# A mixture-of-experts router: small VectorE operations taken out, moved to GpSimd and folded into matmuls

## The chip, the cores and the metric

The kernel runs on one core of a Trainium2 chip. The metric is the device time of one execution in microseconds; lower is better. The core has five engines that run their own instruction streams and wait for one another by semaphores: TensorE (PE, matrix products), VectorE (DVE), ScalarE (ACT), GpSimd (POOL) and SyncE (SP, which here only issues DMAs). Each engine works strictly in the order of its stream, so an instruction that waits holds up all behind it.

## The reference

A block of a transformer in three parts works on 4096 tokens of 256 features: half a feed-forward network, an attention over groups of 64 tokens, and half a feed-forward network again with the same weights. The feed-forward network is a mixture of experts with a shared part:

```python
xn = xf * rsqrt(mean(xf * xf) + eps)              # RMS norm of each token
logits = xn @ router_w.T                          # 8 experts
probs = softmax(logits)
topk_p, topk_i = top_k(probs, 2)                  # two experts for each token
rw = topk_p / sum(topk_p)                         # their weights
order = argsort(~sel, axis=1, stable=True)        # tokens of an expert, in order
dispatch = order[:, :capacity]                    # at most 640 of them
eout = einsum(silu(xg @ rg) * (xg @ ru), rd)      # the expert
routed = zeros.at[dispatch].add(eout * w)
shared = silu(x @ sg) * (x @ su) @ sd
return shared + routed
x = x + 0.5 * ffn(layernorm(x)); x = x + attn(layernorm(x)); x = x + 0.5 * ffn(layernorm(x))
```

The weights of the two experts depend only on the difference of the two largest logits: with d = exp(second - first) they are 1/(1+d) and d/(1+d). The choice of the experts doesn't depend on a positive factor common to a token's logits. A token's place in an expert's list is the number of earlier tokens with the same expert.

## The kernel before

Four stages follow one another: `a` (norm and routing of all tokens for the first network, the shared part of the first four blocks), `b` (the eight experts), `c` (the attention of all tokens, the rest of the shared part, and norm and routing for the second network), `d` (the experts again and the last shared block). A tile is 128 tokens, a block four tiles (512 tokens).

A float32 value is carried as two 16-bit parts, a high and a low one; a product takes the three terms of `TERMS` (high by high, high by low, low by high), added up in one PSUM buffer. `split` makes the two parts of a weight, scaled by `WS` = 16; `project` writes the 3 x 2 matmuls of a product of depth 256.

The shared part (`shared`, `gate_up`, `down`) is what TensorE does most of: for each block 16 chunks, each 12 + 12 matmuls on `pgu` (L306), the activation on ScalarE and VectorE (`sl` L313, L314, L319; `hh` L321, `hl` L322), and 12 matmuls on `po` (L330). The tiles are generators that `drive` runs in small steps between the steps of the shared part. The order that is written down in this way is then planned by the framework's scheduler: it places the instructions on each engine by its own estimate of when each could start. So a change in one place moves other instructions too. Scatters are told to come after the POOL instruction in `self.anchor`.

For each tile, `front_steps` computes mean and variance (L139 to L144; the power on POOL gives `rstd`), the normed tile `X` in two 16-bit parts, transposes it into `xb`, and calls `logits`. There the router weights `rwt` hold their high part in columns 0 to 7 and their low part, scaled by `UP` = 2048, in columns 8 to 15; four matmuls with 16 columns (L207) go through both, and DVE adds the two halves (`q` L211, `L` L212).

When four tiles are there, `route` runs once for the block, in steps:

- the RMS factor `rs` (DVE L220 to L222, the power on POOL L223), and `L` times `rs` (L226);
- the largest values of each tile and their indices (`mx`, `ix` L230, L231), the difference `dl` (L233), its exponential on POOL (L234), the indices as floats `ef` (L236);
- a one-hot `oh` of both choices (L239) and their sum `M` (L243); `C` holds, for each tile of the block, the counts of all tiles before it, partition by partition (L245, L247), `run` the total to date (L248);
- two matmuls on `pp`: a triangle of ones by `M` counts inside the tile (L251), a square of ones by `C` all earlier tiles (L252); VectorE picks the positions (`pk`, `pos` L254, L257), makes the target rows (`df` L260 to L264) and casts them to integers `di` (L266);
- the two weights `w1` and `dl` (L268 to L272);
- for each tile, `scatter`: POOL copies token number, weights and expert into the tile's tag columns (L285) and issues two indirect DMAs (L287) that write the tile's rows to the lists `xg` of the experts.

In stage `c` a tile first goes through the attention (`attn_tile`), and its POOL work shares the queue with the scatters: `ss` (L501, the power for the norms of q and k, which VectorE's `qk` L511 needs), the low parts `xa`, `QK`, `yp`, `e` (L165, L522, L528, L561) and the subtraction of the maximum `S` (L550). The buffers `X` are freed by the scatters; a stage has 10 in `a` and 6 in `c`.

Of the kernel before, what the change touches and what calls it, by code (L numbers as in the profile page):

```python
# [8 lines left out]
F32 = mybir.dt.float32  # L9
F32R = mybir.dt.float32r  # L10
F16 = mybir.dt.float16
BF16 = mybir.dt.bfloat16
# [3 lines left out]
ALU = mybir.AluOpType  # L16
AX = mybir.AxisListType
# [3 lines left out]
P = 128  # L21
# [3 lines left out]
UP = 2048.0  # L25
WS = 16.0
# [3 lines left out]
E = 8  # L30
CAP = 640
LN_EPS = 1e-5
RMS_EPS = 1.1920929e-07
SUBS = ((0, 384), (384, 256))
TERMS = ((0, 0), (0, 1), (1, 0))


class Net:
    def __init__(self, ctx, tc):
        self.tc = tc  # L40
        self.nc = nc = tc.nc
        pool = lambda name, bufs, **k: ctx.enter_context(tc.tile_pool(name=name, bufs=bufs, **k))
        self.cst = pool("cst", 1)
        self.wsh = pool("wsh", 1)
        self.tok = pool("tok", YB)
        self.xb = pool("xb", NB)
        self.xe = pool("xe", 2)
        self.sm = pool("sm", 2)
        self.dr = pool("dr", 1, space=DRAM)
        self.ps_gu = pool("ps_gu", 3, space=PSUM)  # L50
        self.pend = None
        self.anchor = None
        c = self.cst
        self.tri = c.tile([P, P], BF16, name="tri")
        nc.gpsimd.memset(self.tri, 1.0)
        nc.gpsimd.affine_select(
            out=self.tri, in_=self.tri, pattern=[[1, P]], compare_op=ALU.is_gt,
            fill=0.0, base=0, channel_multiplier=-1)
        self.ones = c.tile([P, P], BF16, name="ones")
        nc.gpsimd.memset(self.ones, 1.0)  # L60
        self.iota8 = c.tile([P, E], F32, name="iota8")
        for e in range(E):
            nc.gpsimd.memset(self.iota8[:, e:e + 1], float(e))
        self.mhalf = c.tile([P, 8], F32, name="mhalf")
        nc.gpsimd.memset(self.mhalf, -0.5)
        self.e1 = c.tile([P, 4], F32, name="e1")
        nc.gpsimd.memset(self.e1, 2.718281828459045)
        tk = self.sm.tile([P, 32], I32, name="tk", bufs=1)
        nc.gpsimd.iota(tk, pattern=[[P, 32]], base=0, channel_multiplier=1)
        self.tokid = c.tile([P, 32], F32, name="tokid")  # L70
        nc.vector.tensor_copy(self.tokid, tk)
# [32 lines left out]
    def load_router(self, router_w):  # L104
        nc = self.nc
        r = self.raw.tile([E, H], F32, name="rtr", tag="raw2")
        nc.sync.dma_start(out=r, in_=router_w)
        self.rwt = self.cst.tile([P, 2, 2 * E], F16, name="rwt")
        p = self.m1([P, 2, E], F32, "prt")
        for k in range(2):  # L110
            nc.tensor.transpose(p[:, k, :], r[:, k * P:(k + 1) * P], self.ident[:E, :E])
        z = self.sm.tile([P, 2, E], F32, name="rz", bufs=1)
        nc.vector.tensor_scalar_mul(z, p, UP)
        nc.scalar.mul(self.rwt[:, :, 0:E], z, 1.0 / UP)
        nc.vector.scalar_tensor_tensor(
            out=self.rwt[:, :, E:2 * E], in0=self.rwt[:, :, 0:E], scalar=-UP, in1=z, op0=ALU.mult, op1=ALU.add)

    def load_shared(self, sg, su, sd):

# [82 lines left out]
    def logits(self, fb, t, xt):  # L202

        nc = self.nc
        p = self.m1([P, 2 * E], F32, "pl")
        for a in range(4):
            nc.tensor.matmul(p, lhsT=xt[:, a, :], rhs=self.rwt[:, a % 2, :], start=(a == 0), stop=(a == 3))  # L207
        if t == 0:
            fb["L"] = self.sm.tile([P, 4, E], F32, name="L")
        q = self.sm.tile([P, E], F32, name="q")  # L210
        nc.vector.tensor_scalar_mul(q, p[:, E:2 * E], 1.0 / UP)  # L211
        nc.vector.tensor_tensor(out=fb["L"][:, t, :], in0=q, in1=p[:, 0:E], op=ALU.add)  # L212

    def route(self, R, b, fb):

        nc = self.nc
        sm = self.sm
        mv, rstd = fb["mv"], fb["rstd"]
        rs = sm.tile([P, 4], F32, name="rs")
        nc.vector.tensor_tensor(out=rs, in0=rstd, in1=rstd, op=ALU.mult)  # L220
        nc.vector.tensor_tensor(out=rs, in0=rs, in1=mv[:, :, 1], op=ALU.mult)
        nc.vector.tensor_scalar_add(rs, rs, RMS_EPS * UP ** 2)  # L222
        nc.gpsimd.tensor_tensor(out=rs, in0=rs, in1=self.mhalf[:, :4], op=ALU.pow)  # L223
        yield
        L = fb["L"]
        nc.vector.tensor_tensor(out=L, in0=L, in1=rs.unsqueeze(2).to_broadcast([P, 4, E]), op=ALU.mult)  # L226
        mx = sm.tile([P, 4, E], F32, name="mx")
        ix = sm.tile([P, 4, E], U32, name="ix")
        for t in range(4):
            nc.vector.max(out=mx[:, t, :], in_=L[:, t, :])  # L230
            nc.vector.max_index(out=ix[:, t, :], in_max=mx[:, t, :], in_values=L[:, t, :])  # L231
        dl = sm.tile([P, 4], F32, name="dl")
        nc.vector.tensor_tensor(out=dl, in0=mx[:, :, 1], in1=mx[:, :, 0], op=ALU.subtract)  # L233
        nc.gpsimd.tensor_tensor(out=dl, in0=self.e1, in1=dl, op=ALU.pow)  # L234
        ef = sm.tile([P, 4, 2], F32, name="ef")
        nc.vector.tensor_copy(ef, ix[:, :, 0:2])  # L236
        yield
        oh = sm.tile([P, 4, 2, E], F32, name="oh")
        nc.vector.tensor_tensor(  # L239
            out=oh, in0=ef.unsqueeze(3).to_broadcast([P, 4, 2, E]),  # L240
            in1=self.iota8.unsqueeze(1).unsqueeze(1).to_broadcast([P, 4, 2, E]), op=ALU.is_equal)
        M = sm.tile([P, 4, E], BF16, name="M")
        nc.vector.tensor_tensor(out=M, in0=oh[:, :, 0, :], in1=oh[:, :, 1, :], op=ALU.add)  # L243
        C = sm.tile([P, 4, E], BF16, name="C")
        nc.vector.tensor_copy(C[:, 0, :], R["run"])  # L245
        for t in range(3):
            nc.vector.tensor_tensor(out=C[:, t + 1, :], in0=C[:, t, :], in1=M[:, t, :], op=ALU.add)  # L247
        nc.vector.tensor_tensor(out=R["run"], in0=C[:, 3, :], in1=M[:, 3, :], op=ALU.add)  # L248
        yield
        pp = self.m1([P, 4, E], F32, "pp")  # L250
        nc.tensor.matmul(pp, lhsT=self.tri, rhs=M, start=True, stop=False)  # L251
        nc.tensor.matmul(pp, lhsT=self.ones, rhs=C, start=False, stop=True)  # L252
        pk = sm.tile([P, 4, 2, E], F32, name="pk")
        nc.vector.tensor_tensor(  # L254
            out=pk, in0=oh, in1=pp.unsqueeze(2).to_broadcast([P, 4, 2, E]), op=ALU.mult)
        pos = sm.tile([P, 4, 2], F32, name="pos")
        nc.vector.tensor_reduce(out=pos, in_=pk, axis=AX.X, op=ALU.add)  # L257
        yield
        df = sm.tile([P, 4, 2], F32, name="df")
        nc.vector.scalar_tensor_tensor(  # L260
            out=df, in0=ef, scalar=float(CAP), in1=pos, op0=ALU.mult, op1=ALU.add)
        nc.vector.tensor_scalar(
            out=pos, in0=pos, scalar1=float(CAP), scalar2=8192.0, op0=ALU.is_ge, op1=ALU.mult)
        nc.vector.tensor_tensor(out=df, in0=df, in1=pos, op=ALU.add)  # L264
        di = sm.tile([P, 4, 2], I32, name="di")
        nc.vector.tensor_copy(di, df)  # L266
        w1 = sm.tile([P, 4], F32, name="w1")
        nc.vector.tensor_scalar_add(w1, dl, 1.0)  # L268
        nc.vector.reciprocal(w1, w1)
        nc.vector.tensor_scalar_mul(w1, w1, 0.5 / WS)  # L270
        nc.vector.tensor_tensor(out=dl, in0=dl, in1=w1, op=ALU.mult)
        nc.vector.tensor_tensor(out=w1, in0=w1, in1=dl, op=ALU.subtract)  # L272
        yield
        for t in range(4):
            with self.tc.issue_after(self.anchor.ins) if self.anchor else nullcontext():
                self.scatter(R, b, fb, t, di, w1, dl, ef)
            yield
# [552 lines left out]
```

## Time and profile before

| | before |
|---|---|
| median of 3 runs | 1857.15 us (1856.97 to 1858.42) |
| profiled execution | 1854.02 us |
| its span | 1852.2 us |
| TensorE busy | 1785.9 us (96%) |
| VectorE busy, instructions | 1259.6 us (68%), 3190 |
| ScalarE busy | 940.6 us (51%) |
| GpSimd busy | 726.0 us (39%) |

The profile is of one execution. A line of a group or of the timeline names the line of the kernel, the engine, the operation, output and inputs by the program's names, partitions x elements and type. In the timeline the first two columns are start and duration in microseconds, and the brackets hold the idle time of the engine before the instruction and what ended it. In the table of waits the columns are the total in microseconds, the number of times, and the longest.

### The profile page before, as it was taken

The numbers are of one execution on the slowest core, as the hardware profiler recorded it, in microseconds if no ns is written. First come the engines' busy times: TensorE is split into PE (matmuls) and PEld (weight loads), VectorE is DVE, ScalarE is ACT, GpSimd is POOL, SyncE is SP. The second block draws the span as 40 slices with busy tenths as digits, with TensorE's granted clock in tenths as the row PEclk, the third lists the DMA queues.
The fourth block names the chain that finished last, engine by engine and source line by source line (L and its number), as shares of the span: only waits on it lengthen the run. The fifth ranks groups of instructions, "written<-read, shape, count | busy, mean of one in ns | idle before, by whom it ended". The sixth has DMA issues, their size and how long they took to land.

```text
span 1852.2 us, 37412 instructions
## 1 busy us (share of the span) xinstructions
PE 1785.9 (96%) x13546; PEld 1189.7 (64%) x13546; DVE 1259.6 (68%) x3190; ACT 940.6 (51%) x1991; POOL 726.0 (39%) x943
## 2 busy tenths in 40 slices
PE   6899999999999899999999999999999999999999
PEld 3456557777777556665555656565665677777765
DVE  8666545566666567888888888788765566666643
ACT  4333334555555466666566666666433455555542
POOL 5664430123111334557667575757520011112210
PEclk9999999999999999999999999999999999999999
DMA  9763032555543345657576666756213044445420
GB/s 272 220 161 93 12 78 61 114 121 116 119 107 86 82 81 101 135 104 146 103 140 122 130 130 115 147 104 122 53 34 83 27 106 111 110 109 125 106 47 12
DMA packets 447513, 196.59 MB, mean 106 GB/s; under 512 B 302369, under 2 KB 444381, under 8 KB 447264
## 3 DMA queue, kind: packets, MB, share of 16 engines
q1 hardware_dynamic: 429664, 173.03, 41.6%
q0 software_dynamic: 17664, 21.17, 6.7%
q8 instruction: 106, 1.74, 0.4%
q14 instruction: 79, 0.65, 0.1%
HBM read 81.04 MB, written 52.85 MB: 72 GB/s over the span
## 4 chain that ended last, share of the span: by engine, by line
PE 59%; DVE 11%; POOL 9%; DMA 8%; issue 6%; ACT 4%; SPq 1%; DVEq 0%; POOLq 0%; ACTq 0%
PE pgu L306 38%; PE po L330 19%; POOL xg L287 3%; DVE hl L322 2%; DVE sl L319 2%; DMA xg<-X,di 2%; DVE sl L314 2%; DMA xg<-zero 1%; DMA y<-in_L_attn_x_dram 1%; DMA rs<-in_L_ffn_su_dram 1%; POOL X L285 1%; ACT hh L321 1%; DMA QT<-QK 1%; DVE st L139 1%; ACT V L554 1%
## 5 line engine op out<-in xcount | busy, mean ns | idle before, releaser
L306 PE MATMUL pgu<-xb,sgu 128*128 128x512 f16 x3072 | 740.2, 381 | 19.5 <-DVE sl L314 8.5
L321 ACT CAST hh<-sl 128x512 f16<-128x512 f32 (+2 forms) x512 | 272.8, 533 | 540.8 <-DVE sl L319 535.5
L306 PE MATMUL pgu<-xe,wc 128*128 128x384 f16 (+1 forms) x3072 | 497.1, 299 | 0.6
L306 PEld LDWEIGHTS <-sgu 128*128 128x128 f16 x3072 | 294.1, 98 | 298.1 <-issue 33.0
L319 DVE SCALAR_TENSOR_TENSOR sl<-pgu,sl 128x512 f32<-128x512 f32 (+2 forms) x512 | 300.6, 587 | 203.4 <-PE pgu L306 183.2
L322 DVE TENSOR_TENSOR hl<-sl,hh 128x512 f16<-128x512 f32 (+2 forms) x512 | 328.4, 642 | 146.4 <-ACT hh L321 145.4
L330 PEld LDWEIGHTS <-hh 128*128 128x128 f16 x3328 | 319.6, 98 | 114.8 <-ACT hh L321 18.4
L330 PE MATMUL po<-sdw,hh 128*128 128x256 f16 x2048 | 350.6, 273 | 10.8 <-ACT hh L321 10.0
L306 PEld LDWEIGHTS <-wc 128*128 128x128 f16 x3072 | 300.1, 98 | 94.6 <-issue 2.2
L330 PE MATMUL po<-sdw,hl 128*128 128x256 f16 x1024 | 250.9, 274 | 11.4 <-DVE hl L322 10.6
L330 PE MATMUL po<-wd,hh 128*128 128x256 f16 x1280 | 223.7, 273 | 0.0
L330 PEld LDWEIGHTS <-hl 128*128 128x128 f16 x1664 | 162.6, 98 | 62.3 <-DVE hl L322 28.5
L426 POOL DMA_INDIRECT out_dram<-eo,eid x40 | 64.6, 1616 | 315.2 <-DVE hl L322 247.1
L317 ACT ACTIVATE sl<-pgu 128x384 f32<-128x384 f32 (+1 forms) x336 | 158.8, 473 | 53.8 <-PE pgu L306 30.4
L287 POOL DMA_INDIRECT xg<-X,di x128 | 137.3, 1072 | 89.4 <-DVE di L266 29.9
L426 POOL DMA_INDIRECT acc<-eo,eid x40 | 64.6, 1615 | 261.9 <-DVE hl L322 222.3
L330 PE MATMUL po<-wd,hl 128*128 128x256 f16 x640 | 152.5, 273 | 1.1 <-DVE hl L322 1.1
L314 DVE SCALAR_TENSOR_TENSOR sl<-sl,pgu 128x512 f32<-128x512 f32 x176 | 120.1, 682 | 38.9 <-ACT sl L313 38.2
L100 ACT ACTIVATE wc<-re 128x512 f16<-128x512 f32 x128 | 80.5, 629 | 84.9 <-PE pgu L306 57.4
L313 ACT ACTIVATE sl<-pgu 128x512 f32<-128x512 f32 x176 | 103.9, 591 | 36.5 <-PE pgu L306 35.1
L101 DVE SCALAR_TENSOR_TENSOR wc<-re,wc 128x512 f16<-128x512 f32 x128 | 88.3, 690 | 28.2 <-ACT wc L100 28.0
L550 POOL TENSOR_TENSOR S<-S,amx 128x1024 f32<-128x1024 f32 x32 | 63.7, 1990 | 81.0 <-DVE amx L549 74.1
(140 smaller groups left out, 1718.8 us busy)
## 6 DMA issues: line engine op xcount, KB each, us to landing
re<-in_L_ffn_rg_dram SPq DMA_DIRECT2D x128, 128.0 KB
re<-in_L_ffn_ru_dram SPq DMA_DIRECT2D x128, 128.0 KB
re<-in_L_ffn_rd_dram SPq DMA_DIRECT2D x128, 128.0 KB
xg<-zero SPq DMA_DIRECT2D x16, 650.0 KB
y<-acc SPq DMA_DIRECT2D x64, 128.0 KB
y<-in_L_attn_x_dram SPq DMA_DIRECT2D x32, 128.0 KB
acc<-xr SPq DMA_DIRECT2D x16, 256.0 KB
out_dram<-xr SPq DMA_DIRECT2D x16, 256.0 KB
```

Source lines behind the costliest of these rows:

```text
L100: nc.scalar.mul(hi, src, WS)
L101: nc.vector.scalar_tensor_tensor(out=lo, in0=src, scalar=WS, in1=hi, op0=ALU.mult, op1=ALU.subtract)
L287: i = nc.gpsimd.indirect_dma_start(out=R["xg"][:, :], out_offset=bass.IndirectOffsetOnAxis(ap=di[:, t, k:k + 1], axis=0), in_=X, in_offset ...
L306: nc.tensor.matmul(p, lhsT=wc[:, w, i, k, :], rhs=x[:, 2 * a + k, :], start=(j == 0), stop=(j == 5))
L313: nc.scalar.activation(s, p, AF.Tanh, scale=0.5 / XP)
L314: nc.vector.scalar_tensor_tensor(out=s, in0=s, scalar=1.0, in1=p, op0=ALU.add, op1=ALU.mult)
L317: nc.scalar.activation(s, p, AF.Silu, scale=1.0 / XP)
L319: nc.vector.scalar_tensor_tensor(out=s, in0=ps[1], scalar=1.0 / XP / (2.0 * XP if tanh else 1.0), in1=s, op0=ALU.mult, op1=ALU.mult)
L321: nc.scalar.copy(h[0], s)
L322: nc.vector.tensor_tensor(out=h[1], in0=s, in1=h[0], op=ALU.subtract)
L330: nc.tensor.matmul(o, lhsT=h[a][:, t * P:(t + 1) * P], rhs=wd[:, w], start=(c == 0 and j == 0 and t % 2 == 0), stop=(c == nch - 1 and j == 2),
L426: i = nc.gpsimd.indirect_dma_start(out=R["acc"][:, :], out_offset=bass.IndirectOffsetOnAxis(ap=ids[:, t:t + 1], axis=0), in_=eo, in_offset ...
```

## The change

The logits are computed by `project`: the router weights are split as all others are, high and low part side by side, and the terms add up in the same eight columns, with six matmuls of 8 columns in place of four of 16. ScalarE copies the result from PSUM. The logits keep the factor 16 and are no longer multiplied by `rs`; the factor is put on the difference `dl` instead. The arithmetic of `rs` and of the two weights goes to POOL, with a power of -1 in place of the reciprocal; it stands in one piece behind `dl`, ahead of `ef`. The running sums `C` are gone: three more matmuls with the square of ones add `M` of tile 0, 1 and 2 to the columns of the tiles behind them, and one adds `run`, broadcast over the four tiles; `run` is then updated by a reduction and an addition. `route` has one step less ahead of the scatters.

```diff
@@ load_router
-        self.rwt = self.cst.tile([P, 2, 2 * E], F16, name="rwt")
+        self.rwt = self.cst.tile([P, 2, 2, E], F16, name="rwt")
...
-        z = self.sm.tile([P, 2, E], F32, name="rz", bufs=1)
-        nc.vector.tensor_scalar_mul(z, p, UP)
-        nc.scalar.mul(self.rwt[:, :, 0:E], z, 1.0 / UP)
-        nc.vector.scalar_tensor_tensor(
-            out=self.rwt[:, :, E:2 * E], in0=self.rwt[:, :, 0:E], scalar=-UP, in1=z, op0=ALU.mult, op1=ALU.add)
+        self.split(self.rwt[:, 0], self.rwt[:, 1], p)
@@ logits
-        p = self.m1([P, 2 * E], F32, "pl")
-        for a in range(4):
-            nc.tensor.matmul(p, lhsT=xt[:, a, :], rhs=self.rwt[:, a % 2, :], start=(a == 0), stop=(a == 3))
+        p = self.m1([P, E], F32, "pl")
+        self.project(p, lambda a, k: xt[:, 2 * a + k, :], self.rwt, TERMS)
...
-        q = self.sm.tile([P, E], F32, name="q")
-        nc.vector.tensor_scalar_mul(q, p[:, E:2 * E], 1.0 / UP)
-        nc.vector.tensor_tensor(out=fb["L"][:, t, :], in0=q, in1=p[:, 0:E], op=ALU.add)
+        nc.scalar.copy(fb["L"][:, t, :], p)
@@ route
-        nc.vector.tensor_tensor(out=rs, in0=rstd, in1=rstd, op=ALU.mult)
-        nc.vector.tensor_tensor(out=rs, in0=rs, in1=mv[:, :, 1], op=ALU.mult)
-        nc.vector.tensor_scalar_add(rs, rs, RMS_EPS * UP ** 2)
+        nc.gpsimd.tensor_tensor(out=rs, in0=rstd, in1=rstd, op=ALU.mult)
+        nc.gpsimd.tensor_tensor(out=rs, in0=rs, in1=mv[:, :, 1], op=ALU.mult)
+        nc.gpsimd.tensor_scalar_add(rs, rs, RMS_EPS * UP ** 2)
         nc.gpsimd.tensor_tensor(out=rs, in0=rs, in1=self.mhalf[:, :4], op=ALU.pow)
-        yield
         L = fb["L"]
-        nc.vector.tensor_tensor(out=L, in0=L, in1=rs.unsqueeze(2).to_broadcast([P, 4, E]), op=ALU.mult)
...
         nc.vector.tensor_tensor(out=dl, in0=mx[:, :, 1], in1=mx[:, :, 0], op=ALU.subtract)
+        nc.gpsimd.tensor_tensor(out=dl, in0=dl, in1=rs, op=ALU.mult)
+        nc.gpsimd.tensor_scalar_mul(dl, dl, 1.0 / WS)
         nc.gpsimd.tensor_tensor(out=dl, in0=self.e1, in1=dl, op=ALU.pow)
+        w1 = sm.tile([P, 4], F32, name="w1")
+        nc.gpsimd.tensor_scalar_add(w1, dl, 1.0)
+        nc.gpsimd.tensor_tensor(out=w1, in0=w1, in1=self.mone, op=ALU.pow)
+        nc.gpsimd.tensor_scalar_mul(w1, w1, 0.5 / WS)
+        nc.gpsimd.tensor_tensor(out=dl, in0=dl, in1=w1, op=ALU.mult)
+        nc.gpsimd.tensor_tensor(out=w1, in0=w1, in1=dl, op=ALU.subtract)
...
-        C = sm.tile([P, 4, E], BF16, name="C")
-        nc.vector.tensor_copy(C[:, 0, :], R["run"])
-        for t in range(3):
-            nc.vector.tensor_tensor(out=C[:, t + 1, :], in0=C[:, t, :], in1=M[:, t, :], op=ALU.add)
-        nc.vector.tensor_tensor(out=R["run"], in0=C[:, 3, :], in1=M[:, 3, :], op=ALU.add)
         yield
         pp = self.m1([P, 4, E], F32, "pp")
         nc.tensor.matmul(pp, lhsT=self.tri, rhs=M, start=True, stop=False)
-        nc.tensor.matmul(pp, lhsT=self.ones, rhs=C, start=False, stop=True)
+        for t in range(1, 4):
+            nc.tensor.matmul(pp[:, t:4], lhsT=self.ones, rhs=M[:, 0:4 - t], start=False, stop=False)
+        nc.tensor.matmul(
+            pp, lhsT=self.ones, rhs=R["run"].unsqueeze(1).to_broadcast([P, 4, E]), start=False, stop=True)
+        n4 = sm.tile([P, E], F32, name="n4")
+        nc.vector.tensor_reduce(out=n4, in_=M.rearrange("p t e -> p e t"), axis=AX.X, op=ALU.add)
+        nc.vector.tensor_tensor(out=R["run"], in0=R["run"], in1=n4, op=ALU.add)
...
-        w1 = sm.tile([P, 4], F32, name="w1")
-        nc.vector.tensor_scalar_add(w1, dl, 1.0)
-        nc.vector.reciprocal(w1, w1)
-        nc.vector.tensor_scalar_mul(w1, w1, 0.5 / WS)
-        nc.vector.tensor_tensor(out=dl, in0=dl, in1=w1, op=ALU.mult)
-        nc.vector.tensor_tensor(out=w1, in0=w1, in1=dl, op=ALU.subtract)
         yield
```

More of the change, by code (lines that the diff above doesn't have):

```diff
@@ L65, in __init__ @@
         nc.gpsimd.memset(self.mhalf, -0.5)
+        self.mone = c.tile([P, 4], F32, name="mone")
+        nc.gpsimd.memset(self.mone, -1.0)
         self.e1 = c.tile([P, 4], F32, name="e1")
```

## The prediction

> **What bounds the kernel now.** I read the page's engine table first, then who TensorE waited for between 640 and 1400 us, then one stretch of that stage on three engines.
>
> ```profile
> PE 1785.9 (96%) x13546; PEld 1189.7 (64%) x13546; DVE 1259.6 (68%) x3190; ACT 940.6 (51%) x1991; POOL 726.0 (39%) x943
> PE po L330 <- DVE hl L322: 10.1, 19, 1.2
> PE pgu L306 <- DVE sl L314: 7.3, 14, 0.9
> PE py L572 <- DVE S L544: 3.3, 6, 0.5
> PE py L572 <- DVE qk L511: 2.1, 6, 0.7
> ```
>
> TensorE is busy for 1785.9 of 1852.2 us, so taking work from another engine can win back at most the 66 us in which it stood idle. Some 20 us of those lie in the first 50 us, behind loads. In the attention stage (640 to 1400) it waits for VectorE (DVE) in waits that come 6, 14 and 19 times: a pattern that repeats with each block of four tiles, every 83.6 us. One period:
>
> ```profile
> 1077.62 1.06 POOL L287 DMA_INDIRECT xg<-X,di  x1 [0.29 <-POOL X L285]
> 1078.98 0.97 POOL L287 DMA_INDIRECT xg<-X,di  x1 [0.30 <-issue]
> 1079.97 0.74 POOL L501 TENSOR_TENSOR ss<-ss,mhalf 128x2 f32<-128x2 f32 x1
> ...
> 1098.15 1.55 POOL L287 DMA_INDIRECT xg<-X,di  x1 [0.19 <-issue]
> 1099.73 0.58 POOL L144 TENSOR_TENSOR arstd<-ve,mhalf 128x1 f32<-128x1 f32 x1
> ```
>
> ```profile
> 1080.75 0.88 DVE L511 SCALAR_TENSOR_TENSOR qk<-pqk,ss,lnw 128x256 f32<-128x256 f32 x2 [1.58 <-POOL ss L501]
> ...
> 1100.34 0.16 DVE L152 SCALAR_TENSOR_TENSOR nm<-amv,arstd 128x1 f32<-128x1 f32 x1 [1.55 <-POOL arstd L144]
> ```
>
> ```profile
> 1081.77 0.56 PE L572 MATMUL py<-V,ET 128*128 128x33 f16 x16 [0.26 <-DVE qk L511]
> 1082.87 0.56 PE L572 MATMUL py<-V,ET 128*128 128x33 f16 x16 [0.55 <-DVE S L544]
> 1084.07 0.28 PE L330 MATMUL po<-sdw,hl 128*128 128x256 f16 x1 [0.41 <-DVE hl L322]
> ```
>
> So DVE is not late because it has too much to do: it stands in front of `qk` for 1.58 us until GpSimd (POOL), two scatters late, delivers `ss`. The scatters of the routing are what TensorE waits for here. The three idle times are 0.26, 0.55 and 0.41; each hides about 0.16 more, since a matmul is drawn longer than the distance to the next (0.38 against 0.216 at 512 columns), so this group costs some 1.7 us a block. A second group, behind `arstd`, follows in the next tile.
>
> **The change part by part.** TensorE:
>
> ```profile
> 816.48 0.25 PE L207 MATMUL pl<-rwt,xb 128*128 128x16 f16 x4
> 816.58 0.82 PE L603 MATMUL pao<-wpr,yt 128*128 128x256 f16 x6
> ...
> 1372.20 0.18 PE L251 MATMUL pp<-M,tri 128*128 128x32 bf16 x1
> 1372.23 0.18 PE L252 MATMUL pp<-C,ones 128*128 128x32 bf16 x1
> 1372.26 2.10 PE L306 MATMUL pgu<-xb,sgu 128*128 128x512 f16 x9
> ```
>
> Four logit matmuls hold the array from 816.48 to 816.58, about 26 ns each; a `pp` matmul 30 ns. Eight columns in place of 16 are not shown; 33-column `py` matmuls also stand 25 ns apart, so I take 26 again. Per tile 6 in place of 4: 64 x 2 x 26 ns = 3.3 us; per block 5 in place of 2: 16 x 3 x 29 ns = 1.4 us. Together 4.7; about 0.9 falls into the first 110 us, where TensorE idles anyway. Counted: **+3.8** (0 to +4.7).
>
> VectorE loses, by the group rows, `q` 10.2, `L` 10.6 and 3.0, `rs` 2.4 + 2.5 + 2.7, `C` 5.6 + 7.3, `run` 2.5 and the weights 2.6 + 2.7 + 2.7 + 2.5 + 3.0 = 60 us, and gets a small reduction (as `pos`, 218 ns) and an addition (159 ns) per block, 6 us. These 54 us lie under TensorE. They count only where TensorE waits soon after them: the `q`/`L` pair of the tile after the scatters, 0.33 us in front of a 0.26 wait for `sl`: 0.3 x 7 blocks = **-2.1**; and the first 75 us, where DVE is over 80% busy and 2 blocks lose 20 operations each at about 0.07 us apart: 2.8 us, half counted, **-1.5** (0 to -3).
>
> ScalarE gets 64 copies of 128x8, nearest the 128x16 `rwt` at 217 ns: 13 us on an engine 51% busy. Each stands behind a `sl` that needs a neighbouring matmul group, so **0** (up to +3 if `hh` is held behind one).
>
> GpSimd gets ten instructions per block: nine 128x4 products, sums and scalings, and a power. The power has its row: `dl` L234, 1032 ns. The products have none. POOL subtractions take 684 ns at 256 elements, 1163 at 512, 2133 at 1024; the line through these leaves 0.2 us. Upper bound: a power on one element, 0.60 us (`rstd` L144). The Trainium skill, GPSIMD Engine Reference, section 3 "Performance versus the Vector engine", speaks against the move: a two-input elementwise operation costs GpSimd about twice VectorE's time, which from DVE's 159 ns would make 0.32. I take 0.3, nearer the rows, with the wait of each on the one before. So 9 x 0.3 + 1.0 = 3.7 us a block; by the rule's 0.32 3.9. Where they stand decides. In the planned order the three for `rs` and its power precede `X`, and `ss` behind that: `ss` some 1.2 us later in that tile. There DVE stands 1.07 us idle behind `qk` in front of L314 for ScalarE, and `hl` is now planned ahead of `amx` (1.22 us). The `dl` chain runs among `rstd`, `X`, `xa` and `ss` of the following tile; `ss`, now at 1056.47, comes at about 1058.1, and `hl`, ahead of `qk`, ends at 1057.7 anyway. Both are covered: **0** (to +2.5 us a block, the slow rival).
>
> The same skill, SBUF — State Buffer, "Who interferes with whom", warns of more: a DVE operation with two SBUF inputs and a GpSimd operation reading SBUF shut each other out for a whole instruction. The trace agrees: at 1087.63 `hl` takes 2.54 instead of 0.68, until POOL's `S` ends. If each new POOL instruction held DVE throughout, that would be 60 us of DVE. By the rows it is 794 against 685 ns for `hl` and `sl`, 0.11 us lost at POOL's 66% here; 3.7 us in 83.6 add 4.4 points, so 0.007 x 16 `hl` = 0.1 us a block: left out.
>
> The moved scatters. One step less in the routing makes each come earlier. Now the first pair stands between `X` and `ss`, the last pair around `rstd` and `arstd` of the next tile. In the planned order the first pair stands ahead of `rstd`, in a gap of 2.97 us that POOL idles today (1070.86 to 1073.83); it needs 0.6 of copies and 2 x 1.3, so `rstd` moves by 0.3. `ss` follows `arstd` directly; DVE's input for it is ready once ScalarE squares, now ahead of the other work, so `qk` starts no later than about 1078 instead of 1080.75. The other six follow behind `QK` and `S`. Adding durations, `S` starts at about 1088.1 (now 1087.73), with ScalarE's exponential and an `hh` behind it. So of the first group's 1.7 us I count 1.2, and of the second, whose `arstd` stays behind a full POOL queue, nothing: 6 blocks x 1.2 = **-7.2** (0 to -16).
>
> At the start the second batch of scatters has five zero fills ahead instead of three and comes about 4 us later than 86.09; ScalarE's `X` that waits for it is planned one chunk (3.9 us) later as well: **0** (-3 to +5). At the two stage changes `di` and what follows keep their distance: **0** (+-2).
>
> Sum: 3.8 - 2.1 - 1.5 - 7.2 = -7.0. The profiled execution took 1854.0 (span 1852.2 and 1.8 around it), so 1847.0 there; the median of the runs is 3.1 above it: **1850.1**.
>
> **The rivals.** (1) The change doesn't reach TensorE's waits: `ss` comes earlier, but DVE then waits for `S` or ScalarE, and 7.2 vanishes: 1857.3. For it: `S` on POOL is no earlier. Against: 1.58 us of DVE idle has a named cause that goes. (2) Slower: GpSimd's chain becomes the wait. If small products cost 0.6 us, the two tiles get 2.25 more on top of the uncovered 1.2 (1.65 + 1.2 less 0.55 and 1.07 of DVE idle): 3.5 x 7 = 24, thus 1874. It outweighs the gain from about 0.4 us a product. For it: the 0.60 us row and the rule; against: 128x256 takes only 0.68. (3) The second group goes too: its idle times (0.26, 0.20, 0.87) are 1.3 a block, 8 in all: 1842.
>
> **How the numbers follow.** Likeliest 0.50 (own range 1843 to 1853); rival 1 0.16; rival 2 0.26, anywhere from 1861 to 1874; rival 3 0.08. Leaving a tenth on each side gives 1842 to 1867. A change within 0.2% (3.7 us) can't be told from none: faster 0.56, same 0.16, slower 0.28.
>
> **What would show it.** Right: in the after-profile the idle before `qk` that ends on `ss` falls from 20 us, the `py` waits for `qk` and `S` go, `dl` products show 0.2 to 0.35 us, `pl` stays 26 ns apart. Wrong: `qk` still waiting for `ss` in the tiles of the `rs` and `dl` chains, POOL products of 0.5 us and more, or `hh` waiting for `L`.

## The result and the profile after

The changed kernel takes 1844.2 us (median; 1843.0 to 1847.3), beside 1857.8 for the kernel before on the same chip: ratio 0.9929, 95% interval 0.9912 to 0.9946. By that ratio it is 13.2 us less, with 10.0 to 16.3 as interval. The profiled execution took 1844.2 too, its span is 1842.5 us. (The profiled execution of before, 1854.0, lies 3.8 us under its median, so the two profiles are only 9.7 us apart.)

The page's engine row, and the table of waits of TensorE between 640 and 1400 us (total in us, times, longest):

```profile
PE 1782.8 (97%) x13722; PEld 1197.0 (65%) x13722; DVE 1204.9 (65%) x2869; ACT 952.2 (52%) x2055; POOL 769.5 (42%) x1104
```

```profile
PE pgu L302 <- DVE sl L310: 7.6, 10, 0.9
PE po L326 <- DVE hl L318: 6.1, 9, 1.2
PE po L326 <- ACT hh L317: 2.2, 2, 1.7
```

VectorE has 54.7 us less, GpSimd 43.5 more, ScalarE 11.6 more. (`sl` L314 of before is L310 here, `hl` L318, `po` L326, `py` L568.) The two rows of `py` (the attention's product with V) are gone, and of the 19 and 14 waits for `hl` and `sl` 9 and 10 are left.

To see where the time went I cut both traces at the first and the last `pgu` matmul of the experts and took, for each stage, its length and TensorE's lost time: the distance from matmul to matmul less the distance of undisturbed ones (216, 162 and 109 ns at 512, 384 and 256 columns, 25 to 29 ns for the small ones).

| us | a | b | c | d | sum |
|---|---|---|---|---|---|
| length before | 291.8 | 314.9 | 859.0 | 381.9 | 1847.6 |
| length after | 297.5 | 316.2 | 842.4 | 381.9 | 1838.0 |
| lost before | 34.9 | 1.6 | 45.6 | 4.2 | 86.3 |
| lost after | 38.6 | 2.9 | 26.9 | 4.2 | 72.6 |

The gain is all in stage `c`: 18.7 us less lost, 2.1 us more matmuls. Stage `a` gives 5.7 back, 2.0 of them as matmuls. The period of a block in stage `c` is 80.7 us instead of 83.7. The same part of a period as was shown of before, on GpSimd, VectorE and TensorE:

```profile
1071.29 0.99 POOL L283 DMA_INDIRECT xg<-X,di  x1 [0.30 <-issue]
1072.27 0.61 POOL L142 TENSOR_TENSOR rstd<-ve,mhalf 128x1 f32<-128x1 f32 x1
1072.83 0.57 POOL L142 TENSOR_TENSOR arstd<-ve,mhalf 128x1 f32<-128x1 f32 x1
1073.36 0.87 POOL L497 TENSOR_TENSOR ss<-ss,mhalf 128x2 f32<-128x2 f32 x1
...
1084.90 1.93 POOL L546 TENSOR_TENSOR S<-S,amx 128x1024 f32<-128x1024 f32 x1
```

```profile
1074.27 0.88 DVE L507 SCALAR_TENSOR_TENSOR qk<-pqk,ss,lnw 128x256 f32<-128x256 f32 x2 [0.18 <-POOL ss L497]
...
1083.35 0.69 DVE L318 TENSOR_TENSOR hl<-sl,hh 128x512 f16<-128x512 f32 x1
```

```profile
1078.66 0.96 PE L568 MATMUL py<-V,ET 128*128 128x33 f16 x32
```

`ss` stands directly behind `arstd`, DVE waits 0.18 us for it in place of 1.58, and `qk` starts 4.4 us ahead of `py`, which had waited for it. A second difference is in the last line of DVE: `hl` takes 0.69 us. The `hl` of the same place in before was 2.54 us long, and ended 0.55 us after GpSimd's `S` had ended.

### The profile page after: what moved, and what is told of

Its sections match the earlier page's. It is cut to its first block, busy times and chain, and to the rows that moved or that the text cites. A ratio compares the mean times of both kernels' runs of the same rounds, so it can differ in the third digit from the quotient of the medians.

```text
span 1842.5 us, 37619 instructions
## 1 busy us (share of the span) xinstructions
PE 1782.8 (97%) x13722; PEld 1197.0 (65%) x13722; DVE 1204.9 (65%) x2869; ACT 952.2 (52%) x2055; POOL 769.5 (42%) x1104
## 4 chain that ended last, share of the span: by engine, by line
PE 57%; POOL 12%; issue 11%; DVE 10%; DMA 5%; ACT 4%; SPq 1%; POOLq 0%; DVEq 0%; another core or an unknown queue 0%; ACTq 0%
PE pgu L302 36%; PE po L326 18%; POOL xg L283 3%; DVE sl L315 2%; DVE sl L310 1%; POOL X L281 1%; DVE hl L318 1%; POOL rstd L142 1%; POOL S L546 1%; DMA y<-in_L_attn_x_dram 1%; ACT hh L317 1%; PE pqk L599 1%; ACT sl L309 1%; POOL e L557 1%; DMA xg<-X,di 1%
## 5 line engine op out<-in xcount | busy, mean ns | idle before, releaser
L318 DVE TENSOR_TENSOR hl<-sl,hh 128x512 f16<-128x512 f32 (+2 forms) x512 | 311.0, 608 | 160.1 <-ACT hh L317 153.3
L326 PEld LDWEIGHTS <-hh 128*128 128x128 f16 x3328 | 319.8, 98 | 114.9 <-ACT hh L317 13.9
L326 PE MATMUL po<-sdw,hh 128*128 128x256 f16 x2048 | 349.9, 273 | 10.1 <-ACT hh L317 6.8
L326 PE MATMUL po<-sdw,hl 128*128 128x256 f16 x1024 | 247.5, 273 | 11.7 <-DVE hl L318 10.4
L326 PE MATMUL po<-wd,hh 128*128 128x256 f16 x1280 | 223.6, 273 | 0.0
L326 PEld LDWEIGHTS <-hl 128*128 128x128 f16 x1664 | 162.8, 98 | 57.2 <-DVE hl L318 23.3
L283 POOL DMA_INDIRECT xg<-X,di x128 | 131.3, 1026 | 66.2 <-issue 27.5
L326 PE MATMUL po<-wd,hl 128*128 128x256 f16 x640 | 152.5, 273 | 2.1 <-DVE hl L318 1.9
L310 DVE SCALAR_TENSOR_TENSOR sl<-sl,pgu 128x512 f32<-128x512 f32 x176 | 120.0, 682 | 45.4 <-ACT sl L309 43.2
L102 ACT ACTIVATE wc<-re 128x512 f16<-128x512 f32 x128 | 80.5, 629 | 78.0 <-PE pgu L302 51.2
```

Of the source, the lines that this page charges most:

```text
L283: i = nc.gpsimd.indirect_dma_start(out=R["xg"][:, :], out_offset=bass.IndirectOffsetOnAxis(ap=di[:, t, k:k + 1], axis=0), in_=X, in_offset ...
L310: nc.vector.scalar_tensor_tensor(out=s, in0=s, scalar=1.0, in1=p, op0=ALU.add, op1=ALU.mult)
L318: nc.vector.tensor_tensor(out=h[1], in0=s, in1=h[0], op=ALU.subtract)
L326: nc.tensor.matmul(o, lhsT=h[a][:, t * P:(t + 1) * P], rhs=wd[:, w], start=(c == 0 and j == 0 and t % 2 == 0), stop=(c == nch - 1 and j == 2),
```

## What holds VectorE

That `hl` is one of many. I compared each VectorE instruction of stage `c` with the usual length of its form and added up the excess (over 60 ns): 56.5 us before, 28.6 after. In before, `hl` has 27.4 of it, the routing's `dl` 12.4 and the cast `di` 10.8. In five of the six regular blocks TensorE loses at most 0.12 us at a time behind `dl` for the rest of the block, and b_di below keeps this hold (12.4) and is faster. The cast, of eight numbers a partition, stands in front of the group of waits that the prediction looked at. The kernel before, VectorE and then GpSimd:

```profile
1068.33 0.68 DVE L314 SCALAR_TENSOR_TENSOR sl<-sl,pgu 128x512 f32<-128x512 f32 x1
1068.93 1.97 DVE L266 CAST di<-df 128x8 int32<-128x8 f32 x1
1070.81 0.68 DVE L319 SCALAR_TENSOR_TENSOR sl<-pgu,sl 128x512 f32<-128x512 f32 x1
...
1073.62 0.14 DVE L142 TENSOR_SCALAR ve<-mv 128x1 f32<-128x1 f32 x1
...
1087.63 2.54 DVE L322 TENSOR_TENSOR hl<-sl,hh 128x512 f16<-128x512 f32 x1
```

```profile
1068.74 2.12 POOL L561 TENSOR_TENSOR e<-S,e 128x1024 f16<-128x1024 f32 x1 [0.76 <-ACT e L560]
...
1073.83 0.55 POOL L144 TENSOR_TENSOR rstd<-ve,mhalf 128x1 f32<-128x1 f32 x1 [2.97 <-DVE ve L142]
...
1087.60 0.17 POOL L285 COPY X<-ef 128x1 f32<-128x1 f32 x1
1087.73 1.89 POOL L550 TENSOR_TENSOR S<-S,amx 128x1024 f32<-128x1024 f32 x1
```

`di` starts 0.19 us after GpSimd's `e` and ends with it, 1.97 us later; in the other kernels it takes 0.15 to 0.17 us where it isn't held. The Trainium skill, SBUF — State Buffer, "Who interferes with whom", has such a rule for VectorE operations with two SBUF inputs and for those in a two-port mode, which a cast can enter: whichever is issued first has the pair of ports shared with GpSimd for its whole instruction, and the other is blocked. The lengths agree; that this cast ran in a two-port mode no run shows by itself. The `hl` at 1087.63 starts 0.10 us ahead of `S` and is held all the same: it starts 0.03 us behind the copy, and `S` follows the copy without a gap. Behind `di` wait `y`, the statistics and `ve`; GpSimd stands idle 2.97 us for `ve`; then come `rstd`, `X`, two scatters, and `ss`. So what made `ss` late has two parts: the scatters ahead of it (the prediction's cause) and a chain that begins 1.8 us late for one held cast. Which of the two the change took away was the question of the experiments.

For each run the table gives the ratio to the kernel before with its 95% interval, the lengths of stages `a` and `c`, the length of `di` in the six regular blocks of stage `c` (the median; b_logits has 1.97 in the first, bl_halves 1.05 in the last), by how much `qk` starts ahead of `py` there, and the time that VectorE was held in stage `c` (all in us, from the profiled execution). The differences given as "measured" below are the ratio times the median of the kernel before in the same series, which lay between 1852.7 and 1860.0 us; the expectations of the later runs have somewhat other figures for the earlier ones (12.3 for a_yield, 15.1 for b_logits).

| kernel | ratio | a | c | `di` | `qk` ahead | held |
|---|---|---|---|---|---|---|
| before | 1 | 291.8 | 859.0 | 1.97 | 1.0 | 56.5 |
| changed | 0.9929 (0.9912 to 0.9946) | 297.5 | 842.4 | 0.17 | 4.4 | 28.6 |
| b_noyield | 1.0018 (1.0009 to 1.0027) | 296.4 | 859.0 | 0.16 | 3.8 | 57.7 |
| a_yield | 0.9939 (0.9925 to 0.9953) | 295.4 | 840.6 | 0.16 | 3.1 | 47.0 |
| a_dve | 0.9920 (0.9906 to 0.9933) | 295.1 | 841.6 | 0.17 | 4.5 | 26.7 |
| b_halves | 0.9913 (0.9900 to 0.9927) | 288.1 | 844.6 | 0.16 | 5.2 | 23.5 |
| b_di | 0.9975 (0.9967 to 0.9983) | 297.3 | 849.5 | 0.17 | 2.1 | 45.9 |
| ay_late2 | 0.9978 (0.9968 to 0.9988) | 296.0 | 848.6 | 0.15 | 1.8 | 55.0 |
| b_counts | 1.0024 (1.0014 to 1.0034) | 293.4 | 860.1 | 1.97 | 1.0 | 63.1 |
| b_logits | 0.9914 (0.9898 to 0.9929) | 288.3 | 842.5 | 0.16 | 2.8 | 49.1 |
| b_pool | 0.9963 (0.9949 to 0.9976) | 293.9 | 852.4 | 1.97 | 4.3 | 60.3 |
| bl_halves | 0.9925 (0.9911 to 0.9939) | 289.6 | 843.8 | 0.16 | 2.6 | 48.8 |
| a_halves | 0.9938 (0.9924 to 0.9951) | 297.8 | 839.4 | 0.17 | 4.4 | 24.7 |
| a_counts | 0.9922 (0.9909 to 0.9936) | 295.8 | 846.9 | 0.17 | 3.5 | 29.8 |

## The experiments

The first four compared the missing step (the moved scatters) with the arithmetic.

**b_noyield**, the kernel before without the step:

```diff
         nc.gpsimd.tensor_tensor(out=rs, in0=rs, in1=self.mhalf[:, :4], op=ALU.pow)
-        yield
         L = fb["L"]
```

> The kernel before with one line less: the step that separated the power of rs from the scaling of L. Every instruction is the old one; the scatters of a block come one step earlier in the written order. Step theory (the earlier scatters make the whole gain, the new arithmetic none): stage c loses what it lost in the changed kernel, some 19 us less than before, TensorE has none of the 4.7 us of extra matmuls, VectorE keeps its 54 us of small operations (2 to 4 us of cost): 1840 to 1846 us. In the trace the waits of py for qk and S are gone and hl is never held over 2 us. Arithmetic theory (fewer small VectorE operations make the gain): 1854 to 1860, hl and py wait as before.

Measured: 3.3 us slower. The step theory falls. The scatters did move ahead and `qk` comes 3.8 us ahead of `py`, as the prediction had it; the waits of `py` are gone. But `psc` (the product of q and k) waits for `qk` now, and `po` for ScalarE; stage `c` is as long as before. Table of waits of TensorE:

```profile
PE po L329 <- ACT hh L320: 8.7, 7, 1.4
PE po L329 <- DVE hl L321: 6.7, 16, 1.2
PE psc L540 <- DVE qk L510: 5.5, 6, 0.9
```

Here another instruction is held: an `hl` ahead of the statistics, 1.89 us long in each block.

**a_yield**, the changed kernel with the step put back:

```diff
         nc.gpsimd.tensor_tensor(out=rs, in0=rs, in1=self.mhalf[:, :4], op=ALU.pow)
+        yield
         L = fb["L"]
```

> The changed kernel with that step put back, all of its new arithmetic kept. Step theory: the waits of py for qk and S and the hl of 2 us and more are back, and with 4.7 us of extra matmuls the time is 1856 to 1863 us. Arithmetic theory: 1842 to 1848, as the changed kernel.

Measured: 11.3 us below the kernel before, near the changed kernel. So the gain doesn't need the step, though the scatters stand ahead of `ss` again, in before's order. Here `di` (VectorE) starts 0.02 us after `e` (GpSimd) and isn't held:

```profile
1062.58 0.16 DVE L269 CAST di<-df 128x8 int32<-128x8 f32 x1
```

```profile
1062.56 2.17 POOL L558 TENSOR_TENSOR e<-S,e 128x1024 f16<-128x1024 f32 x1 [0.73 <-ACT L L207]
```

Counted from the block's first `pp`, `ve` comes at 5.98 us (8.49 before) and `ss` at 12.43 (14.84): 2.4 us earlier, with the same two scatters ahead of it. But two `hl` are 2.48 and 1.92 us long here too. Those holds cost TensorE little when all comes 2.4 us earlier.

**a_dve**, the changed kernel with `rs` and the weights on VectorE again:

```diff
-        nc.gpsimd.tensor_tensor(out=rs, in0=rstd, in1=rstd, op=ALU.mult)
+        nc.vector.tensor_tensor(out=rs, in0=rstd, in1=rstd, op=ALU.mult)
...
+        nc.vector.tensor_scalar_add(w1, dl, 1.0)
+        nc.vector.reciprocal(w1, w1)
```

> The changed kernel with the arithmetic of rs and of the two weights on VectorE again, at its old places and with the reciprocal; the product of dl with rs and the scaling by 1/16 are on VectorE too, one step less as in the changed kernel. Step theory: no part of the gain comes from GpSimd's new work; stage c stays as in the changed kernel, and stage a, which got 3.6 us slower, regains 0 to 3.6 if GpSimd's chain was its cause: 1840 to 1846 us. Arithmetic theory (relief of VectorE): half of VectorE's relief is undone, 1848 to 1853.

Measured: 14.8 us below, not to be told from the changed kernel. In the changed kernel the moved arithmetic brings nothing and costs nothing that can be measured.

**b_halves**, the kernel before with GpSimd's two large subtractions in two instructions each:

```diff
-        self.anchor = nc.gpsimd.tensor_tensor(
-            out=S, in0=S, in1=mx.unsqueeze(2).to_broadcast([P, 16, 64]), op=ALU.subtract)
+        for q in range(0, 16, 8):
+            self.anchor = nc.gpsimd.tensor_tensor(
+                out=S[:, q:q + 8], in0=S[:, q:q + 8],
+                in1=mx[:, q:q + 8].unsqueeze(2).to_broadcast([P, 8, 64]), op=ALU.subtract)
```

> The kernel before with the two large GpSimd subtractions, S and e, as two instructions of 512 elements each in place of one of 1024; what is computed is the same. Theory of the shared port (hl, 2.54 and 1.93 us long in two places of each block, is held until the GpSimd instruction that overlaps it ends): hl is held for half as long at most, 1.2 to 1.6 us, and of the four TensorE waits in the middle of a block (0.19, 0.42, 0.52, 0.37 us) 0.7 to 1.1 us go: 1849 to 1854 us. Rival (hl is long for another reason, or TensorE waits there for ScalarE's exponential): hl stays over 1.9 us or the waits stay, 1856 to 1860.

Measured: 16.1 us below, twice what I expected and more than the change itself, with no edit of the routing. The halves did not do it in the way I thought (see bl_halves). They made the scheduler plan another order in stage `c`, in which `ss` stands ahead of the scatters, and `di` starts 0.07 us ahead of `e`; `qk` is 5.2 us ahead of `py`. Its order in stages `a` and `b` is that of the kernel before, instruction by instruction.

The next four tested the held cast and took the change's parts alone.

**b_di**, the kernel before with the last addition writing the integers:

```diff
-        nc.vector.tensor_tensor(out=df, in0=df, in1=pos, op=ALU.add)
         di = sm.tile([P, 4, 2], I32, name="di")
-        nc.vector.tensor_copy(di, df)
+        nc.vector.tensor_tensor(out=di, in0=df, in1=pos, op=ALU.add)
```

> The kernel before with one small VectorE operation less in the routing of a block: the last addition of the target rows writes the integers di itself, and the cast that made di is gone; all else is the kernel before. Theory of the one held instruction: in the kernel before the cast di starts 0.18 us after GpSimd's e in six blocks and is held to its end, 1.97 us instead of 0.16, and the statistics of the next tile, rstd, the scatters, ss, qk and py all come 1.8 us later for it. Now the last write of di stands ahead of e (under 0.3 us long in the trace): the waits of py for qk and S shrink or go, stage c loses 8 to 20 us less, and the time is 7 to 16 us below the kernel before. Rival (the work on VectorE as a whole counts; 16 operations less are 3 us of 1260): within 2 us of the kernel before.

Measured: 4.6 us below; the mechanism as expected, the total missed. `di` takes 0.17 us, `ve` comes 1.5 us earlier, the waits of `py` are gone, and stage `c` is 9.5 us shorter. Stage `a`, whose order had changed as well, is 5.5 longer.

**ay_late2**, a_yield with two additions of 0 ahead of `di`:

```diff
+        for _ in range(2):
+            nc.vector.tensor_scalar_add(df, df, 0.0)
         nc.vector.tensor_copy(di, df)
```

> The changed kernel with the step put back (a_yield, 12.3 us faster than the kernel before) and two additions of 0 on VectorE ahead of the cast di, 16 x 2 operations, some 6 us of VectorE work in all. In a_yield di started 0.02 us after e and took 0.16 us. Theory of the one held instruction: di or one of the two is now held to the end of e (1.5 to 2.1 us in six blocks), py waits for qk and S again, and 7 to 14 us of the gain are lost: 2 us above to 6 us below the kernel before. Rival (relief of VectorE as a whole): at most 1 us lost, 10 to 13 us below the kernel before.

Measured: 4.1 us below the kernel before, so 7.2 of a_yield's 11.3 are lost, as the held instruction has it. The second addition (VectorE) is caught by `e` (GpSimd):

```profile
1067.20 0.17 DVE L270 TENSOR_SCALAR df<-df 128x8 f32<-128x8 f32 x1
...
1067.99 1.39 DVE L270 TENSOR_SCALAR df<-df 128x8 f32<-128x8 f32 x1
```

```profile
1067.18 2.17 POOL L560 TENSOR_TENSOR e<-S,e 128x1024 f16<-128x1024 f32 x1 [0.73 <-ACT L L207]
```

`ve`, `ss` and `S` all come 1.33 to 1.34 us later than in a_yield, and the period grows by 1.4 us, from 80.5 to 81.9. One detail was wrong: it isn't `py` that waits. `qk` is still 1.8 us ahead of it; the waits are for `hl`, whose holds now count. TensorE's waits for `hl`, first a_yield, then ay_late2:

```profile
PE po L327 <- DVE hl L319: 2.5, 3, 1.2
```

```profile
PE po L329 <- DVE hl L321: 8.4, 16, 1.2
```

**b_counts**, the running sums alone:

```diff
-        for t in range(3):
-            nc.vector.tensor_tensor(out=C[:, t + 1, :], in0=C[:, t, :], in1=M[:, t, :], op=ALU.add)
...
+        for t in range(1, 4):
+            nc.tensor.matmul(pp[:, t:4], lhsT=self.ones, rhs=M[:, 0:4 - t], start=False, stop=False)
```

> The kernel before with only the running sums of the change: C and its copies gone, three more small matmuls, run updated by a reduction and an addition. Five operations of VectorE less in the step ahead of pp, two more (0.38 us) between pp and the cast di, and 1.4 us more of TensorE. Theory of the one held instruction: the time follows what di shows. If di is about 0.17 us long, the time is 8 to 16 us below the kernel before; if it is still held for 1.5 us or more, it is within 3 us of it. Rival (relief of VectorE as a whole): some 4 us below the kernel before, a third of the gain as it is a third of the relief, whatever di shows.

Measured: 4.4 us slower. `di` is held for 1.97 us in the same six blocks, and `py` waits as before:

```profile
PE py L573 <- DVE S L545: 3.3, 6, 0.5
PE py L573 <- DVE qk L512: 2.9, 6, 0.8
```

VectorE is relieved and TensorE gets nothing of it: this relief as such is worth nothing. Of the 4.4 us 1.4 are the added matmuls; where the rest goes isn't settled.

**b_logits**, the logits alone:

```diff
-        for a in range(4):
-            nc.tensor.matmul(p, lhsT=xt[:, a, :], rhs=self.rwt[:, a % 2, :], start=(a == 0), stop=(a == 3))
+        self.project(p, lambda a, k: xt[:, 2 * a + k, :], self.rwt, TERMS)
...
-        nc.vector.tensor_scalar_mul(q, p[:, E:2 * E], 1.0 / UP)
-        nc.vector.tensor_tensor(out=fb["L"][:, t, :], in0=q, in1=p[:, 0:E], op=ALU.add)
+        nc.scalar.copy(fb["L"][:, t, :], p)
```

> The kernel before with only the logits of the change: six matmuls of 8 columns in place of four of 16, the copy from PSUM on ScalarE in place of q and L on VectorE; L is still scaled by rs, and the factor 16 is taken out in the base of the exponential. TensorE has 3.3 us more. Theory of the one held instruction: the time follows what di shows. If di is about 0.17 us long, the time is 6 to 14 us below the kernel before; if it is held for 1.5 us or more, it is 1 us below to 5 above. Rival (relief of VectorE as a whole): some 3 us below the kernel before, whatever di shows.

Measured: 15.9 us below, as much as the whole change or more, though TensorE has 128 matmuls more. The run holds its own control: in the first block `di` is caught, from the second on it is 0.02 us ahead of `e`. The first block is 82.3 us long, the four behind it 80.5 to 80.9. VectorE, then GpSimd:

```profile
815.09 1.97 DVE L259 CAST di<-df 128x8 int32<-128x8 f32 x1
...
897.17 0.16 DVE L259 CAST di<-df 128x8 int32<-128x8 f32 x1
```

```profile
814.90 2.13 POOL L554 TENSOR_TENSOR e<-S,e 128x1024 f16<-128x1024 f32 x1 [0.76 <-ACT L L205]
...
897.19 2.13 POOL L554 TENSOR_TENSOR e<-S,e 128x1024 f16<-128x1024 f32 x1 [0.76 <-ACT L L205]
```

`ve` comes at 5.95 us, another 1.06 earlier than in b_di: `q` and `L` no longer stand between `di` and `y`, and both statistics go ahead of an `hl`.

The last four asked whether parts and repairs add up.

**b_pool**, the GpSimd part alone (the step kept):

```diff
-        nc.vector.tensor_tensor(out=L, in0=L, in1=rs.unsqueeze(2).to_broadcast([P, 4, E]), op=ALU.mult)
...
+        nc.gpsimd.tensor_tensor(out=dl, in0=dl, in1=rs, op=ALU.mult)
...
+        nc.gpsimd.tensor_tensor(out=w1, in0=w1, in1=self.mone, op=ALU.pow)
```

> The kernel before with only the GpSimd part of the change: rs and the two weights on GpSimd, the scaling of L by rs replaced by a product on dl; logits and running sums as before, and the step kept. Theory of the held instruction: q and L still stand ahead of the statistics, so the time follows from di: 8 to 14 us below the kernel before if di is about 0.17 us long, 2 below to 6 above if it is held. From the three parts alone (logits 15.1 below, running sums 4.4 above, the changed kernel 13 below) a sum that adds up would leave this part 2.5 us above. Rival (VectorE's relief as a whole, 144 operations less): some 5 us below whatever di shows.

Measured: 6.9 us below with `di` held: the theory of the one held instruction is not the whole, and here it missed. (The sum in the expectation has the wrong sign: 15.1 below and 4.4 above leave this part 2.5 below, not above.) The planned order on GpSimd has changed, and no scatter stands ahead of `ss`:

```profile
1155.73 0.56 POOL L146 TENSOR_TENSOR rstd<-ve,mhalf 128x1 f32<-128x1 f32 x1 [3.63 <-DVE ve L144]
1156.39 0.56 POOL L146 TENSOR_TENSOR arstd<-ve,mhalf 128x1 f32<-128x1 f32 x1
1158.41 0.70 POOL L503 TENSOR_TENSOR ss<-ss,mhalf 128x2 f32<-128x2 f32 x1 [1.46 <-DVE ss L501]
...
1162.13 1.11 POOL L289 DMA_INDIRECT xg<-X,di  x1 [0.17 <-POOL QK L524]
```

That is the prediction's mechanism, on its own: `ve` comes 0.9 us later than in before and `ss` 2.6 us earlier.

**bl_halves** and **a_halves** put the two halves into b_logits and into the changed kernel:

> The kernel before with the logits of the change (b_logits) and with S and e on GpSimd in two instructions each (b_halves); the order up to stage c is that of b_logits. In b_logits TensorE still waits twice a block, 0.95 us for an hl that yp and e hold for 2.96 us, and 0.88 us behind the statistics of the attention. Theory of the held instruction: hl is held for at most 1.5 us, the first of the two waits goes, 0.95 x 6 to 7 = 6 us: 19 to 24 us below the kernel before. Rival (the two edits win the same time): 14 to 18 below.

> The changed kernel with S and e on GpSimd in two instructions each. In the changed kernel no hl is held over 1.4 us, but TensorE waits twice a block (1.03 and 0.87 us) behind rstd and arstd, which stand behind e. Theory of the held instruction: little is left to win; two halves take 0.2 us longer than one whole, so the two waits stay or grow by 0.2 to 0.6 us: 10 to 15 us below the kernel before. Rival (shorter instructions let rstd and arstd in between): both waits shrink by half, 18 to 22 below.

Measured: 13.9 and 11.5 us below. In bl_halves the rival (14 to 18 below) comes nearest, and the trace shows why: two halves back to back hold VectorE as one. VectorE, then GpSimd:

```profile
1162.57 3.10 DVE L315 TENSOR_TENSOR hl<-sl,hh 128x512 f16<-128x512 f32 x1
```

```profile
1162.20 0.70 POOL L161 TENSOR_TENSOR yp<-Y,yp 128x256 f16<-128x256 f32 x1
1162.83 2.28 POOL L557 TENSOR_TENSOR e<-S,e 128x512 f16<-128x512 f32 x2
1165.04 0.67 POOL L278 COPY X<-tokid 128x1 f32<-128x1 f32 x1
```

`hl` gets in when `e` ends, past two boundaries between GpSimd instructions. In a_halves stage `c` is 3.0 us shorter than in the changed kernel (the wait of 1.03 is 0.79), but the ratio doesn't tell the two apart.

**a_counts**, the changed kernel with the running sums of before:

```diff
-        for t in range(1, 4):
-            nc.tensor.matmul(pp[:, t:4], lhsT=self.ones, rhs=M[:, 0:4 - t], start=False, stop=False)
...
+        nc.tensor.matmul(pp, lhsT=self.ones, rhs=C, start=False, stop=True)
```

> The changed kernel with the running sums C as before: the part that alone was 4.4 us slower than the kernel before is undone, logits and GpSimd part stay, and the step stays out. Theory (what a part is worth is set by where TensorE then waits, not by the part itself): stage c holds the same two waits a block as the changed kernel, TensorE has 1.4 us less, VectorE 11 us more that lie under TensorE: 11 to 16 us below the kernel before. Rival (the parts add up): 4.4 us better than the changed kernel, 17 to 19 below.

Measured: 14.5 us below. The part that alone cost 4.4 us brings at most 1 to 2 when it is taken out of the changed kernel. Each of step, GpSimd part and running sums can be undone alone with the time within 2 us of the changed kernel's, inside the intervals. The four parts alone do come to a sum near the whole (3.3 + 4.4 - 15.9 - 6.9 = -15.1, beside -13.2), but this says little: the GpSimd part is 6.9 of it and can be undone without a loss that shows. The changed kernel without its logits was not run. So it stays open whether the logits, which alone win as much as the whole, carry the gain there too.

What follows together: in the regular blocks `py` waits where `qk` is 1.0 us ahead of it, and no longer where it is 1.8 or more ahead. Two ways lead there: `di` escapes `e` (b_logits, a_yield, b_di), or `ss` stands ahead of the scatters (b_pool). That a held instruction in front of `ve` costs time is shown by ay_late2 against a_yield and by the first block of b_logits. The lead of `qk` is not all: b_noyield has 3.8 and is slower, with other waits. The changed kernel has both ways, since its `di` ends 1.8 us before the next `e` starts; how its gain divides between them is not shown. No kernel tried is shown to be faster than the changed one; five have lower ratios with overlapping intervals.

Open stays stage `a`. The changed kernel's 297.5 us return in a_halves, which has the same order there (297.8), so they belong to the program; b_logits and bl_halves, also of one order, have 288.3 and 289.6. But before and b_halves, again of one order, differ by 3.7. No single part carries the 5.7: each kernel with the step gone, the running sums or the GpSimd part has 293 to 298, and b_di, with none of them, 297.3. Why b_logits has one wait of 0.95 us in the middle of a block where b_di has four (1.5 us together) isn't settled beyond its `S` being 0.7 us earlier.

## Why the prediction was right or wrong

**Direction and range held, the named cause in part, and part of it is luck.** 1844.2 lies in 1842 to 1867 and in the likeliest case's 1843 to 1853; the gain is about twice the 7.0 counted. The waits named did go, but the term that was to carry the gain, the moved scatters, is not needed for it: a_yield puts them back and is still 11.3 us below.

**TensorE: right.** +3.8 was counted; the stages `a` and `c` show 2.0 and 2.1. The `pl` of a tile stand 25 ns apart.

**VectorE at the start: right in sign.** The first 60 us lose 15.9 instead of 18.5, 2.6 us against the 1.5 counted. The pair `q`/`L` elsewhere was put at 2.1, for 0.3 us in front of one wait. Alone, with its six matmuls, it moved stage `c` by 16.5: the 0.3 us counted not by themselves but for the order that was planned without them, in which `di` starts ahead of GpSimd's `e` and `ve` comes 2.5 us earlier. That way was not in the working. And on the way that was, the pair did not stand on the path: between `L` and that `sl` VectorE is idle for ScalarE, which waits for GpSimd's `S` (the kernel before):

```profile
1091.23 0.69 DVE L314 SCALAR_TENSOR_TENSOR sl<-sl,pgu 128x512 f32<-128x512 f32 x1 [0.66 <-ACT sl L313]
```

```profile
1089.65 1.06 ACT L558 ACTIVATE S<-S 128x1024 f32<-128x1024 f32 x1 [1.62 <-POOL S L550]
```

**ScalarE's copies and GpSimd's products: right.** The copies take 159 ns on average, GpSimd's nine products 0.20 to 0.33, 0.26 on average against 0.3, the power of -1 1.07. Three of the groups (busy us, mean ns):

```profile
L232 POOL TENSOR_TENSOR w<-w,mone 128x4 f32<-128x4 f32 x16 | 17.1, 1066 | 0.3
...
L217 POOL TENSOR_SCALAR rs<-rs 128x4 f32<-128x4 f32 x16 | 5.3, 333 | 0.9
...
L235 POOL TENSOR_TENSOR w<-w,dl 128x4 f32<-128x4 f32 x16 | 3.2, 201 | 1.3
```

The slow rival at 0.6 is out, and a_dve shows that the chain is covered.

**The moved scatters: the mis-sized step.** `qk` starts "about 1078 instead of 1080.75" was right: counted from `psc`, it comes 2.5 us earlier. The whole 1.7 us of the first group went, where I counted 1.2. But six blocks of 1.7 are 10; stage `c` lost 18.7 less. The rest are four waits in the middle of the block, of 0.19, 0.42, 0.52 and 0.37 us, 1.5 a block. The likeliest case counted of them only the `q`/`L` pair in front of the second; rival 3 had the second and the fourth, by their idle times of 0.26 and 0.20. The first and the third stand behind two held `hl`, the second behind ScalarE, whose `sl` comes after the exponential that waits 1.62 us for GpSimd's `S`. The first `hl` is free in the changed kernel because `S` comes *later* with respect to it, 1.55 us behind its start and not 0.10; the second because it starts 0.82 us ahead of `yp` and `e`, not 0.78 behind the start of `e`. With the later `S` the exponential, too, comes after that `sl`. The fourth stands behind `arstd`, for which VectorE waits 1.55 us in before, and in the changed kernel, where no scatter stands between `rstd` and `arstd`, 0.36. I had read the late `S` as the end of the gain. The reading that `hl` is held "until POOL's `S` ends" was right for its end; the hold began with the copy ahead of `S`.

**The exclusion of the ports: left out at 0.1 us a block, and wrong in kind.** I spread GpSimd's extra time over `hl` as a mean. The rule that I cited speaks of whole instructions, and the groups of before had it, a mean of 843 ns for a cast of eight numbers:

```profile
L266 DVE CAST di<-df 128x8 int32<-128x8 f32 x16 | 13.5, 843 | 0.2
```

What counts is who starts first, by 0.02 to 0.2 us, and what stands behind. The change took VectorE's held time from 56.5 to 28.6 us, while I had expected it to grow.

**The second group: right for its two large waits.** They (1.03 and 0.87 us) are in the changed kernel unchanged, now behind `e` rather than scatters. The small ones that rival 3 counted to this group went, as said above.

**Scatters at the start and stage changes: 0 was counted, +6.3 was lost** in the rest of stage `a`, with 1.3 in `b`. The first is past the 5 I allowed; the same order of stage `a` differs by 3.7 between two executions (before and b_halves), so its size is uncertain.

**That the scatters are the cause: one way of two.** b_noyield, which moves them alone, is slower; b_pool, where the planned order frees `ss` of them while `di` stays held, wins 6.9; a_yield wins 11.3 with them in their old place.

## What to carry to other kernels

Look in the groups for a mean that is far too long for its shape, and in the timeline for what that instruction overlaps: a small VectorE instruction that starts just behind a long GpSimd one can be held for the rest of it, and all that stands behind with it. It matters only where TensorE then waits: the mean that is most out of proportion here, 923 ns for the four numbers of `dl`, had in five of six blocks none over 0.12 us behind it. A fifth of a microsecond of work ahead of it can be worth ten times that per period, in either sign; so the worth of an edit is that of the order it produces, and must be measured with the other edits in place. Before crediting a part with a gain, undo it alone: here each of three parts could go without a loss that shows, and two of them by themselves were a loss.

## What the runs showed of the hardware

The hold is all or nothing at a scale of 0.2 us and less: a cast that starts 0.02 us after GpSimd's `e` takes 0.16 us (a_yield), one 0.19 us after it 1.97 (before); `dl`, another operation, is held from 0.05 us on (2.1 us long in b_counts, 0.15 where it is free). Cutting a GpSimd instruction in two doesn't let VectorE in between when the two follow at once: `hl`, 3.10 us long, waited past `yp` and both halves of `e`. It goes the other way as well: GpSimd's copy of one element takes 0.67 us instead of 0.17 when it meets the `hl` that has just got in. Not held in the same places are VectorE's statistics (0.73 us inside `e` in a_yield) and `sl`, which reads PSUM.
